# A two-layer graph network on one core: sums copied back over what they sum, and a reordered beginning

## The chip, the cores and the metric

The kernel runs on one core of a Trainium2 chip. The metric is the device time of one execution in microseconds (us); each kernel is run several times and the median is used. The engines are named as in the profile: PE is TensorE (matmuls; PEld are its weight loads), DVE is VectorE, ACT is ScalarE, POOL is GpSimd, and SP is SyncE, which here only issues transfers. Every engine works through its own list of instructions in order. Transfers issued by SP run on queue q1, those issued by POOL on queue q0; both share 16 DMA engines.

## The reference

`x` has 16 graphs of 1024 nodes with 256 channels; `adj` is one 1024 x 1024 matrix. All is float32.

```
h   = relu(layernorm(x))
c   = mean over channels of h                       # one number a node
Wg  = adj * A_s(c_m - c_n)                          # 1024 x 1024 for each graph
q   = relu((h^T Wg) * para)^T ;  k, v = h @ kv_w    # 4 heads of 64
x   = x + softmax(q k^T * scale) v
h   = relu(layernorm(x))
h1  = relu(batchnorm((A_hat h) @ W1^T + b1))        # statistics over all graphs
out = x + batchnorm(h1 @ W2^T + b2)
```

The softmax is taken without its maximum: exponentials are multiplied with the values, summed beside that, and the quotient is formed at the end.

## The kernel before, in words

The Python code emits all instructions itself, in the order in which each engine is to run them (`tc.manual_schedule()`); waits follow from the tiles' buffers. A pool with n buffers of a tag hands them round, and the first write into a reused buffer waits for the last use of its former tile.

**The beginning** (the `else` branch at the end of `layers`) is not overlapped with attention. `load_x(0)` brings graph 0 in two halves, after the small `vec`. `Norm` takes two row tiles at a time through `stats` (DVE), `scale` (POOL), `shift` (DVE) and `relu` (ACT), and `relu` also sums the channels into `csum`. `transposed` makes h^T on PE (L385) with a DVE copy (L388), half by half. `keys_values` is a generator of eight pieces: four products for the keys `pk` with an ACT copy each (L613), two for the first half of the nodes and two for the second, and four pieces for the values `pv` with DVE copies (L630). `differences(0)` spreads `csum` along rows: DVE copies (L190), PE transposes `cbp_c` (L201), ACT copies into `cbc` (L202). `weigh` then makes eight tiles `w`: absolute difference and tanh on ACT (L439, L447), product with a loaded tile of `adj` on DVE (L426), and for graph 0 a row sum of that tile (L429). `AHEAD = 6` steps of it are woven into the remaining pieces of `keys_values`. Then graphs 1 and 2 are loaded, and `plain_queries(0)` (16 pieces, `pg` and `q`, L593 and L596) runs with the rest of `weigh` and the first layer norm of graph 1 woven in from piece 5. `weave(main, (start, side))` takes one step of a side after every piece from number `start` on; what is left of a side follows the main part.

**Attention** runs over 64 units (graph, pair of heads `k`, half of the queries `f`), four steps each. A step emits `scores` (PE L871, exponential on ACT L879), `add` (DVE L898 and L901 add the exponentials into `acc`, two buffers), `values` of the step before (PE L912), and pieces of a background. When a unit ends, `sums` adds up `acc` over its partitions on PE (L929), copies the result to `row` on ACT (L931), and POOL stores it (L932) and loads it back, turned, as `inv` (L937). Two or three steps later `finish` transposes the unit's output and `add_output` takes the reciprocal of `inv` on DVE (L955) and adds the result to `x`.

The tile `row` comes from the pool `py`, which has four buffers under the tag `y`. Others use the same tag:

```python
                two = py.tile([P, 2, HB], F32, tag="y", name=f"two_{u}")
                one = py.tile([P, HB], F32, tag="y", name=f"one_{u}")
                y = py.tile([P, FB], F32, tag="y", name=f"y_{i}_{j}")
```

`two` and `one` belong to `graph()`, which runs once, in the background of graph 0: POOL loads blocks of `adj` (`au`, L247), combines them (L261 to L271) and writes them to DRAM (`aht_d`, L273 to L275), eight rounds in all. `degrees()` runs beside it: SP loads `at` (L206), ACT and DVE sum it (L221 to L229), and POOL takes a root (L84). All POOL work of these and of the units' sums stands in one queue.

Of the kernel before, what the change touches and what calls it, by code (L numbers as in the profile page):

```python
# [10 lines left out]
F32 = mybir.dt.float32  # L11
# [6 lines left out]
P = 128  # L18
# [5 lines left out]
def gnn_two_layers_kernel(  # L24
# [12 lines left out]
    nc = tc.nc  # L37
    B, N, C = x.shape
    H1 = w1_t.shape[1]
    NT = N // P  # L40
# [3 lines left out]
    FB = 512  # L44
# [10 lines left out]
    ident = const.tile([P, P], F32, name="ident")  # L55
# [1 line left out]
    neg_half = const.tile([P, NT], F32, name="neg_half")  # L57
    nc.gpsimd.memset(neg_half, -0.5)
    vec = const.tile([P, 18], F32, name="vec")
    nc.sync.dma_start(out=vec, in_=vecs)  # L60
    b1, g1, be1 = (vec[:, i * HC : (i + 1) * HC] for i in range(3))
    b2, g2, be2 = (vec[:, 3 * HC + i * CC : 3 * HC + (i + 1) * CC] for i in range(3))
    stats1 = const.tile([P, HC, B * NH, 6], F32, name="stats1")
# [22 lines left out]
    def layers(shifted):  # L86
# [13 lines left out]
        py = st.enter_context(tc.tile_pool(name=f"py_{kind}", bufs=4))  # L100
# [29 lines left out]
        def run(*parts):  # L130
            for part in parts:
                while advance(part) is not None:
                    pass
            while queue:
                queue.pop(0)()

        def weave(main, *sides):

            for i, cost in enumerate(main):
                for start, side in sides:  # L140
                    if i >= start:
                        cost += next(side, 0.0)
                yield cost
            for _, side in sides:
                yield from side
# [7 lines left out]
        def bank(name):  # L153
            return ps_mm.tile([P, FB], F32, tag="mm", name=name)
# [4 lines left out]
                r = slice(e * HW, (e + 1) * HW)  # L159
                nc.tensor.matmul(dst[r], left[:, r], right, start=start, stop=stop)  # L160

        def load_x(b):
            xs[b] = p3.tile([P, NT, C], F32, tag="x", name=f"x_{b}")
            for half in range(2):
                t = slice(half * NT // 2, (half + 1) * NT // 2)
                nc.sync.dma_start(
                    out=xs[b][:, t], in_=x[b].rearrange("(t p) c -> p t c", p=P)[:, t]
                )
# [8 lines left out]
            )  # L177
            return t

        load_x(0)  # L180
        kvw = const.tile([P, CC, 2 * C], F32, tag="kvw", name=f"kvw_{kind}")
        nc.sync.dma_start(out=kvw, in_=kv_w.rearrange("(k p) j -> p k j", p=P))
        rows = big.tile([P, NH, NT], F32, name="rows")
# [190 lines left out]
        def transposed(b, k, halves=range(NH)):  # L374

            h = hs["a", b]
            if 0 in halves:
                ht = p3.tile([P, N], F32, tag="ht", name=f"ht_{b}_{k}")
                hts.setdefault(b, []).append(ht)
            ht = hts[b][k]  # L380
            for g in halves:
                pt = bank(f"htp_{b}_{k}_{g}")
                for j in range(FB // P):
                    t = g * (FB // P) + j
                    nc.tensor.transpose(  # L385
                        pt[:, j * P : (j + 1) * P], h[:, t, k * P : (k + 1) * P], ident
                    )
                nc.vector.tensor_copy(ht[:, g * FB : (g + 1) * FB], pt)  # L388

        def differences(b):  # L390


            cbc = p1.tile([P, N], F32, tag="cbc", name=f"cbc_{b}")
            cbcs[b] = (
                cbc.rearrange("p (t q) -> p t q", t=NT)
                if b == 0
                else cbc.rearrange("p (q t) -> p t q", t=NT)
            )
            weighers[b] = weigh(b)
            if b == 0:  # L400
                broadcast_row(cbc, columns_of(csums[b], f"c{b}"), f"c{b}")
                return
            nc.sync.dma_start(out=csum_d[b].rearrange("(p t) -> p t", p=P), in_=csums[b])
            nc.sync.dma_start(
                out=cbc, in_=csum_d[b].rearrange("(o n) -> o n", o=1).to_broadcast([P, N])
            )
# [161 lines left out]
        def plain_queries(b):  # L568

            h = hs["a", b]  # L570
            qs[b] = [p4.tile([P, N], F32, tag="q", name=f"q_{b}_{k}") for k in range(CC)]
            for q in range(NH):
                cols = slice(q * FB, (q + 1) * FB)
                pgs = [bank(f"pg_{b}_{q}_{k}") for k in range(CC)]
                paras = []
                for k in range(CC):
                    paras.append(p2.tile([P, FB], F32, tag="para", name=f"para_{b}_{q}_{k}"))
                    nc.sync.dma_start(out=paras[k], in_=para[k * P : (k + 1) * P, cols])
                for th in range(NP):
                    i = q * NP + th  # L580
                    for k in range(CC):
                        for j in range(TH):
                            t = th * TH + j
                            product(
                                pgs[k],
                                h[:, t, k * P : (k + 1) * P],
                                weighted[b][i][:, j, :],
                                t == 0,
                                t == NT - 1,
                            )  # L590
                        if th == NP - 1:
                            dst = qs[b][k][:, cols]
                            nc.vector.tensor_mul(dst, pgs[k], paras[k])  # L593

                            soon(
                                lambda dst=dst: nc.scalar.activation(  # L596
                                    dst, dst, AF.Relu, scale=SCALE
                                )
                            )
                        yield 1.71  # L600
# [282 lines left out]
        class Unit:  # L883
# [39 lines left out]
            def sums(self):  # L923

                u = self.index
                pt = ps_t.tile([P, FB], F32, tag="t", name=f"sums_{self.name}")
                for e in range(2):
                    r = slice(e * HD, (e + 1) * HD)
                    nc.tensor.matmul(pt[r, :], ones, self.acc[:, e, :], start=True, stop=True)  # L929
                row = py.tile([P, FB], F32, tag="y", name=f"row_{self.name}")  # L930
                nc.scalar.copy(row, pt)  # L931
                nc.gpsimd.dma_start(  # L932
                    out=sums_d[u], in_=row.rearrange("(e r) c -> e r c", r=HD)[:, 0, :]
                )
                self.inv = p2.tile([P, FB // P, 2], F32, tag="inv", name=f"inv_{self.name}")
                for e in range(2):
                    nc.gpsimd.dma_start(  # L937
                        out=self.inv[:, :, e], in_=sums_d[u][e].rearrange("(j q) -> q j", q=P)
                    )
# [85 lines left out]
        with st:  # L1025
            if shifted:
                for b in range(B):
                    if b > 0:
                        load_x(b)
                    run(Norm(b, True).all())  # L1030
                    differences(b)
                    for k in range(CC):
                        transposed(b, k)
                    run(islice(weighers[b], AHEAD))
                    run(weave(plain_queries(b), (0, weighers[b])))
                    if b == 0:
                        run(degrees(), graph())
                        load_later()
                    run(keys_values(b))
                    shifted_attention(b)  # L1040
                    norm = Norm(b, False)
                    run(norm.all())
                    nc.gpsimd.dma_start(out=x1_d[b], in_=xs[b])
                    if b == B - 1:
                        attn.close()
                        turns.append(second(kind))
                    run(aggregate(b), hidden(b))
            else:
                norm = Norm(0, True)
                norm.stats(0, 1)  # L1050
                norm.scale(0, 2)
                for t in range(2, NT, 2):
                    norm.stats(t, t + 1)
                    norm.shift(t - 2, 2)
                    norm.relu(t - 2, t - 1)
                    norm.scale(t, 2)
                norm.shift(NT - 2, 2)
                norm.relu(NT - 2, NT - 1)
                products = keys_values(0)

                for k in range(CC):
                    transposed(0, k, (0,))
                run(islice(products, 2))
                for k in range(CC):
                    transposed(0, k, (1,))
                differences(0)
                run(weave(products, (0, islice(weighers[0], AHEAD))))
                load_x(1)
                load_x(2)
                run(weave(plain_queries(0), (0, weighers[0]), (5, Norm(1, True).all())))  # L1070
                attention()
                attn.close()
                turns.append(second(kind))
                run(aggregate(B - 1), hidden(B - 1))
# [324 lines left out]
```

## Time and profile before

| | us |
|---|---|
| median of three runs | 2637.73 (2637.07 to 2638.66) |
| the profiled execution | 2634.44, of which its span 2632.6 |
| PE busy | 2555.9 (97% of the span) |
| DVE, ACT, POOL busy | 1725.3, 1440.5, 547.9 |

The busy share of PE is an average over a beginning, a long steady part and an end. The view of stretches gives busy time by engine and the granted PE clock for chosen times; the view of waits tells what ended idle time; the timeline gives single instructions with the idle time ahead of them in brackets. Times in these views count from the start of the span.

### The profile page before, as it was taken

What the parts mean: (1) busy time and instruction counts of PE and PEld (TensorE: products, weight loads), DVE (VectorE), ACT (ScalarE), POOL (GpSimd) and SP (SyncE); (2) the same over time, 40 slices, a digit from 0 to 9 for tenths busy, and PEclk for the clock granted to TensorE, in tenths of its full rate; (3) what the DMA queues carried; (4) which work ended last, traced back from release to release, by engine and by line L of the source; (5) the groups of instructions that cost most, each with busy time, mean ns of one, the idle gap of its engine ahead of it and who ended that gap; (6) DMA issues with size and microseconds to landing.
All of it is one profiled execution on the core that took longest, in us unless ns stands there. A gap on an engine that the chain in (4) does not pass through costs nothing. (4 is left out here: it accounts for less than half of the span.)

```text
span 2632.6 us, 31894 instructions
## 1 busy us (share of the span) xinstructions
PE 2555.9 (97%) x11754; PEld 937.9 (36%) x11754; DVE 1725.3 (66%) x2736; ACT 1440.5 (55%) x1905; POOL 547.9 (21%) x648
## 2 busy tenths in 40 slices
PE   8979999999999999999999999999999999999995
PEld 3333333333333333333333333333333333334443
DVE  5647575766757675757667575757576675557675
ACT  5756464737364564647374645556464744335544
POOL 1361111011111111110111111111111112036653
PEclk9999999999999999999999999999999999999997
DMA  4463415252433324152524343342425233455559
GB/s 162 136 214 104 153 61 181 84 179 82 152 101 141 104 97 148 59 186 77 180 81 152 101 150 102 109 135 66 176 73 180 81 137 97 132 196 207 193 182 378
DMA packets 137188, 364.02 MB, mean 138 GB/s; under 512 B 21440, under 2 KB 38336, under 8 KB 130880
## 3 DMA queue, kind: packets, MB, share of 16 engines
q1 hardware_dynamic: 110272, 282.70, 31.5%
q0 software_dynamic: 26752, 79.20, 8.7%
q8 instruction: 95, 1.56, 0.3%
q14 instruction: 69, 0.57, 0.1%
HBM read 287.06 MB, written 74.78 MB: 137 GB/s over the span
## 5 line engine op out<-in xcount | busy, mean ns | idle before, releaser
L879 ACT ACTIVATE p<-sc 128x1024 f32<-128x1024 f32 x512 | 495.0, 1020 | 470.3 <-PE sc L871 464.1
L901 DVE TENSOR_TENSOR acc<-acc,p 128x1024 f32<-128x1024 f32 x384 | 470.8, 1226 | 222.4 <-ACT p L879 202.1
L871 PE MATMUL sc<-q,k 64*128 64x512 f32 x2048 | 511.4, 618 | 14.3 <-ACT p L879 14.3
L912 PE MATMUL o<-p,v 128*64 128x512 f32 x2048 | 497.0, 606 | 0.0
L160 PE MATMUL pg<-w,h_a 128*64 128x512 f32 x1600 | 358.1, 592 | 3.6 <-ACT k L613 1.9
L160 PE MATMUL pa<-aht,h_b 128*64 128x512 f32 x1536 | 343.5, 592 | 0.0
L871 PEld LDWEIGHTS sc<-q,k 64*128 64x128 f32 x2048 | 176.2, 186 | 336.8 <-issue 278.7
L439 ACT ACTIVATE w<-cbc,csum 128x512 f32<-128x512 f32 x256 | 293.5, 1198 | 0.0
L932 POOL DMA_DIRECT2D sums_d<-row x64 | 37.6, 587 | 1199.8 <-ACT row L931 1199.8
L160 PE MATMUL py<-at,w 128*64 128x512 f32 x1024 | 230.4, 592 | 0.0
L912 PEld LDWEIGHTS o<-p,v 128*64 128x64 f32 x2048 | 124.6, 136 | 294.6 <-issue 293.9
L426 DVE SCALAR_TENSOR_TENSOR w<-w,adj 128x1024 f32<-128x1024 f32 x128 | 157.9, 1234 | 89.2 <-ACT w L447 85.2
L160 PEld LDWEIGHTS pg<-w,h_a 128*64 128x64 f32 x1600 | 115.6, 137 | 231.7 <-issue 216.9
L160 PEld LDWEIGHTS pa<-aht,h_b 128*64 128x64 f32 x1536 | 110.4, 137 | 213.3 <-issue 201.0
L726 ACT ACTIVATE y<-py,vec 128x512 f32<-128x512 f32 x128 | 87.7, 685 | 149.0 <-PE py L160 125.1
L730 DVE BATCH_NORM_STATS2 stats<-y 128x6 f32<-128x512 f32 x128 | 85.5, 687 | 86.2 <-ACT y L726 86.2
L898 DVE TENSOR_TENSOR acc<-p,p 128x1024 f32<-128x1024 f32 x64 | 78.9, 1232 | 92.3 <-ACT p L879 92.3
L447 ACT ACTIVATE w<-w 128x1024 f32<-128x1024 f32 x128 | 135.2, 1056 | 1.8
L501 DVE TENSOR_TENSOR w<-w,w 128x1024 f32<-128x1024 f32 x112 | 132.9, 1218 | 1.5
L727 POOL DMA_DIRECT2D y_d<-y x128 | 70.2, 549 | 303.3 <-ACT y L726 302.1
L937 POOL DMA_DIRECT2D inv<-sums_d x128 | 98.4, 772 | 147.0 <-issue 63.3
L160 PEld LDWEIGHTS py<-at,w 128*64 128x64 f32 x1024 | 74.2, 137 | 145.2 <-issue 139.5
(151 smaller groups left out, 2822.0 us busy)
## 6 DMA issues: line engine op xcount, KB each, us to landing
aht<-aht_d SPq DMA_DIRECT2D x224, 512.0 KB, 6.3
adj<-in_adj_dram SPq DMA_DIRECT2D x128, 512.0 KB, 4.2
y_d<-y POOLq DMA_DIRECT2D x128, 256.0 KB, 2.6
yin_f<-y_d SPq DMA_DIRECT2D x32, 1024.0 KB, 6.3
x<-in_x_dram SPq DMA_DIRECT2D x32, 512.0 KB, 5.0
para<-in_para_dram SPq DMA_DIRECT2D x64, 256.0 KB, 3.9
x_d<-x POOLq DMA_DIRECT2D x16, 1024.0 KB, 10.4
xo_f<-x_d SPq DMA_DIRECT2D x32, 512.0 KB, 8.6
```

The source lines that it names most:

```text
L160: nc.tensor.matmul(dst[r], left[:, r], right, start=start, stop=stop)
L426: nc.vector.scalar_tensor_tensor(w, w, 1.0, a, op0=ALU.add, op1=ALU.mult)
L439: nc.scalar.activation(w[:, t, :].rearrange("p (t q) -> p t q", q=P), cbc[:, q * NT // NH : (q + 1) * NT // NH], AF.Abs, bias=csum[:, th * ...
L447: nc.scalar.activation(made[i], made[i], AF.Tanh, scale=-0.5 / C)
L501: nc.vector.tensor_sub(block(i)[part], block(x)[part], block(y)[part])
L726: nc.scalar.activation(y, made, AF.Identity, bias=b1[:, j : j + 1])
L730: nc.vector.bn_stats(stats1[:, j, i, :], y)
L871: nc.tensor.matmul(sc[:, e, :], ks[b][k][r, m * P : (m + 1) * P], qs[b][k][r, f * FB : (f + 1) * FB], start=True, stop=True,)
L879: nc.scalar.activation(pr, sc, AF.Exp)
L901: nc.vector.tensor_add(self.acc, self.acc, pr)
L912: nc.tensor.matmul(self.o[r, :], vs[b][k][:, m, r], pr[:, e, :], start=(m == 0), stop=(m == NT - 1),)
L937: nc.gpsimd.dma_start(out=self.inv[:, :, e], in_=sums_d[u][e].rearrange("(j q) -> q j", q=P))
```

## The change

It has five parts. The result of `sums` is copied into the first half of `acc` itself instead of a tile of `py`. At the very beginning PE transposes the identity 24 times into an unused bank. The input of graph 0 comes in four transfers of two row tiles instead of two of four, and `vec` is loaded after it and after `kvw`. The two pieces of `keys_values` for the second half of the nodes come ahead of `differences(0)` instead of behind it. The first layer norm of graph 1 is woven in from piece 10 of `plain_queries(0)` instead of piece 5; by the emitted order its last four row tiles then come to ACT behind the last queries, the last two of them directly ahead of the first exponential.

```diff
-    nc.sync.dma_start(out=vec, in_=vecs)
...
-        def load_x(b):
+        def load_x(b, parts=2):
             xs[b] = p3.tile([P, NT, C], F32, tag="x", name=f"x_{b}")
-            for half in range(2):
-                t = slice(half * NT // 2, (half + 1) * NT // 2)
+            for part in range(parts):
+                t = slice(part * NT // parts, (part + 1) * NT // parts)
...
-        load_x(0)
+        load_x(0, 4)
...
-                row = py.tile([P, FB], F32, tag="y", name=f"row_{self.name}")
+                row = self.acc[:, 0, :]
                 nc.scalar.copy(row, pt)
...
             else:
+                nc.sync.dma_start(out=vec, in_=vecs)
+
+                warm = bank("warm")
+                for i in range(24):
+                    j = i % (FB // P)
+                    nc.tensor.transpose(warm[:, j * P : (j + 1) * P], ident, ident)
                 norm = Norm(0, True)
...
                     transposed(0, k, (1,))
+                run(islice(products, 2))
                 differences(0)
                 run(weave(products, (0, islice(weighers[0], AHEAD))))
                 load_x(1)
                 load_x(2)
-                run(weave(plain_queries(0), (0, weighers[0]), (5, Norm(1, True).all())))
+                run(weave(plain_queries(0), (0, weighers[0]), (10, Norm(1, True).all())))
```

## The prediction

> **What bounds the kernel now.** I read the page's first part, then the view of stretches, the waits of PE and ACT, and the timelines around them.
>
> ```profile
> PE 2555.9 (97%) x11754; PEld 937.9 (36%) x11754; DVE 1725.3 (66%) x2736; ACT 1440.5 (55%) x1905; POOL 547.9 (21%) x648
> ```
>
> ```profile
> 0.00:60.00 60.00, 47.48 (x242) 20.01 (x244) 33.61 (x71) 33.51 (x65) 7.09 (x20) 1.00 0.44 150
> 60.00:104.00 44.00, 38.28 (x168) 12.68 (x166) 22.70 (x37) 35.40 (x47) 2.52 (x4) 0.96 0.37 119
> 104.00:200.00 96.00, 82.06 (x394) 30.01 (x392) 54.37 (x78) 55.41 (x71) 68.43 (x91) 0.95 0.61 203
> 328.00:2296.00 1968.00, 1965.65 (x9358) 693.34 (x9356) 1311.92 (x2069) 1087.61 (x1423) 286.72 (x394) 1.00 0.36 120
> ```
>
> The columns are length, busy time of PE, PEld, DVE, ACT and POOL, the PE clock, DMA. From 328 to 2296 us PE idles 2.4 us: nothing is to be had there. The change can touch 12.5 idle us before 60, 5.7 before 104 and 13.9 before 200. In the last of these POOL is busy 68.4 of 96 us, far above its share elsewhere.
>
> ```profile
> ACT row L931 <- POOL two L266: 13.4, 1, 13.4
> ACT row L931 <- DMA aht_d<-two: 8.9, 1, 8.9
> ```
>
> Twice the copy to `row` waits for a `py` buffer that `graph()` holds. ACT's exponentials stand behind it, and PE waits 1.69 us at 142.5 and 8.22 at 181.1. Now POOL, and what DVE and PE do with its result:
>
> ```profile
> 142.88 0.58 POOL L275 DMA_DIRECT2D aht_d<-one  x1
> 143.46 0.58 POOL L932 DMA_DIRECT2D sums_d<-row  x1
> 151.38 1.56 POOL L937 DMA_DIRECT2D inv<-sums_d  x2 [7.34 <-DMA sums_d<-row]
> ...
> 183.79 1.68 POOL L84 TENSOR_TENSOR deg<-deg,neg_half 128x8 f32<-128x8 f32 x1
> 185.44 0.64 POOL L932 DMA_DIRECT2D sums_d<-row  x1
> 187.43 1.54 POOL L937 DMA_DIRECT2D inv<-sums_d  x2 [1.35 <-DMA sums_d<-row]
> ```
>
> ```profile
> 193.26 0.20 DVE L955 RECIPROCAL inv<-inv 128x8 f32<-128x8 f32 x1
> ...
> 194.96 2.54 DVE L901 TENSOR_TENSOR acc<-acc,p 128x1024 f32<-128x1024 f32 x2
> ```
>
> ```profile
> 198.35 1.03 PE L929 MATMUL sums<-acc,ones 128*64 128x512 f32 x4
> ```
>
> The row copied at 138.9 is stored at 143.46, the one copied at 179.5 at 185.44: each time as soon as POOL ends the work ahead of it (L275, L84), without a wait for ACT. **POOL, not the copy, decides when `inv` returns.** DVE needs it at L955, L901 stands behind L955, and PE's next `sums` needs L901.
>
> **What the skill says.** The Trainium skill, "TensorE: Matmul & The Clock Gate", Part 1 (the clock gate), says that PE runs at half clock until a free-running window of about 3.4 us was busy, and again after an idle one. The trace agrees: `pk` begins at 11.58 and its weight loads come 0.86 us apart until 14.2, 0.43 from 14.87; after the 8.22 us wait the `sc` group takes 3.79 us instead of 1.99. Its Part 4 (PE-mode transpose) says that transposes don't count as busy. The trace differs: from 2564 to 2598, where PE does transposes alone (L1325), the clock is 0.99. So I let the 24 raise it. Part 1 also says that ACT and DVE are strict FIFO, as the stalls behind L931 and L955 show.
>
> **Part by part.** Input: without `vec` ahead, the first issue comes at 0.73 instead of 1.18 (0.45 us), and 262 KB of the 524 need not land first, at the 368 GB/s of 3.5 to 5.5 us another 0.7 to 0.9. The first stats start 1.33 earlier (5.43 before) and the first relu, R, at 6.44 instead of 7.77. Two more issues of 0.5 us and `vec` delay `kvw` by 0.5 and the first `adj` by 1.0 on SP; `adj` isn't used before 26.7.
>
> Idle transposes: they begin at about 1.5, when the identity is there. 16 at half clock took 3.67 us at the end (0.23 each), so 24 need at most 5.5 and end by 7.0, when the first real one could start (R + 0.75 = 7.2): no delay. But real transposes come only every 0.59 us with ACT until about R + 2.4, so the clock may fall again. With it full, the first keys end at R + 7.05; if a window falls, about R + 8.4; before R + 8.98.
>
> Keys ahead: 2 x 1.72 us of `pk` now stand ahead of `cbp_c`, while DVE's `cb_c` copies hide beside them. Counting on from the first keys: eight transposes and two copies to +2.15 (0.74 a copy), second keys from +1.4 to +4.85, ACT copy 0.6, last `cbp_c` at +6.05. It ends at R + 13.1 = 19.5, or 20.9; before 20.36. In DVE's order three `v` copies now stand ahead of the first L426: product three ends 5.45 after `cbp_c`, copy 0.75, L426 and L429 2.35, so the first `adj` buffer is free 8.55 later; before 29.06 - 20.36 = 8.7. That releases the fourth `adj`, the loads of x and para, and the fifth `adj`, for which DVE waited until 41.72. These bytes (3.67 MB) keep the queue full, so the 41.72 moves with it: earlier by 0.95, or later by 0.4.
>
> Layer norm behind: two pairs of stats (0.96 each) leave DVE's way after 41.72, and `q` is ready 6.25 later instead of 7.55. Of ACT's eight relus (0.59 each) the last two now stand just ahead of the first exponential: 1.2 us. From 41.72 to that exponential I get 6.25 + 12.24 (seven `pg` pieces) + 1.4 (L593, L596) + 1.2 = 21.1; before 21.15. **Nothing is gained.** Behind it on SP, `csum_d`, `cbc` and the next `adj` come 5 us later than 57.6 to 59.4; first used at 75.9 and 79.4, so hidden. Without that cover each us late would be one on ACT.
>
> So the beginning is worth s = 0, between -1 and +1. Up to 104 ACT sets the pace (35.4 of 44 us) and carries s on.
>
> Sums: both copies go at once; the 8.9 and 13.4 us end. `acc` is now held until POOL's store lands, and DVE's first add two units later waits for that: store landed by 151.4, next use 165.7, hidden by 14 us, and by 10 where 187.4 meets 197.8. Between 104 and 185 POOL's chain needs no result of the late copies, so it ends at 185.44 - s again. Its `inv` lands 2.9 us after the issue at 188.2: 191.1. From L955 to the end of L901 were 4.24 us, so `sums` runs at 195.35 instead of 198.35: **3.0 us gained, not the 12 of the stalls.** PE, with the 9.5 idle and 2.1 slow us behind 172.8 gone, is there by about 187 and waits 8 us: **what is late next is `inv`.** After such a wait the clock is down for half to one and a half windows, 0.9 to 2.6 us lost, I take 1.7. The `at` loads, no longer held by ACT, move from 140 to 146 up to 132 to 139: they may shorten the 7.34 us wait at 151.38 or lengthen POOL's waits for `au` before. I take 0.3 gained, bounds -2.7 and +6.0 (the wait falling to the 1.35 of the next row).
>
> Sum: 0 + 3.0 - 1.7 + 0.3 = 1.6 us. The profiled execution took 2634.44, 3.3 under the median of the runs; I take the difference over to the median: 2636.1.
>
> **The rivals.** *POOL gives way* (chance 0.23): the sums store meets no `at` loads, all 6.0 us come back, PE waits 2 to 3 us only and loses 0.8 of clock: 3.0 + 6.0 - 0.8 = 8.2, so 2629.5. For it: three `at` loads lie in that wait now. Against: `cbc` and two `adj` loads follow them on SP and move up into their place. *POOL's chain grows* (0.13): two `at` loads of 524 KB at 383 GB/s (5.5 to 11 us) put 2.7 us ahead of `au`, the beginning loses 0.8, the clock 2.5: 3.0 - 2.7 - 0.8 - 2.5 = -3.0, 2640.7. It decides from where delay and clock exceed the 3.0; more than 5.3 would need both windows of the first keys cold too. *The beginning does nothing and the copy still waits* (0.02): 2637.7; in the emitted order it waits for PE alone. My forecast, **POOL's queue sets the end**, has 0.62 and its own range 2632.5 to 2639.5.
>
> **The numbers.** A measurement here can tell about 0.2% (5.3 us) from no change. Faster by that: most of the first rival and an edge of mine, 0.24; slower: the tail of the second, 0.07; between: 0.69. The range reaches from the first rival to the second, 2629.5 to 2640.7.
>
> **What would show it.** Right: no ACT wait at L931, but a DVE wait of 6 us or more for `inv` at L955 near 185 and a PE wait at `sums` L929 near 190 with a dip of the clock; POOL's third L932 within 2 us of 185.4; the first exponential within 1 us of 62.9. Wrong: PE idle under 3 us between 160 and 200, or a first exponential before 60.

## The result, and the profile after

The changed kernel takes 2641.99 us (median of 14 runs, 2640.22 to 2645.14), the kernel before on the same chip 2637.6 (2634.14 to 2638.66). The ratio is 1.0018, with an interval of 1.0011 to 1.0026: **slower, by 4.4 us in the medians**, where 1.5 us of gain were forecast. The profiled execution took 2640.84, of which its span 2638.9. Line numbers in views of the changed kernel and of runs made from it are its own, mostly one less than before; those of runs made from the kernel before (`e1`, `e4`, `e9`, `e10`, `e13`, `e15`, `e17`, `e18`) are its.

The first part of the page, and the view of stretches with the columns of before:

```profile
PE 2562.8 (97%) x11778; PEld 943.3 (36%) x11778; DVE 1728.1 (65%) x2736; ACT 1441.1 (55%) x1905; POOL 551.4 (21%) x648
```

```profile
0.00:60.00 60.00, 52.56 (x276) 24.17 (x278) 34.92 (x72) 33.27 (x63) 7.10 (x20) 1.00 0.44 150
60.00:104.00 44.00, 37.13 (x164) 12.40 (x162) 22.05 (x35) 37.11 (x53) 3.17 (x5) 0.96 0.36 120
104.00:200.00 96.00, 78.85 (x380) 29.26 (x378) 53.10 (x75) 53.88 (x67) 71.28 (x91) 0.93 0.61 203
328.00:2296.00 1968.00, 1965.51 (x9362) 694.19 (x9362) 1313.16 (x2069) 1090.46 (x1426) 287.26 (x395) 1.00 0.36 120
```

The long part from 328 us is as it was. PE is busy 5.1 us longer before 60, and most of that are the idle transposes. The loss is between 104 and 200: PE idles 17.2 us instead of 13.9, its clock is lower, and POOL is busier by 2.9 us. The waits of that stretch, PE's and DVE's (total, times, longest):

```profile
PE sums L928 <- DVE acc L900: 17.9, 2, 9.5
```

```profile
DVE inv L954 <- DMA inv<-sums_d: 22.2, 2, 13.1
```

ACT's waits for a buffer at the copy are gone; in their place DVE waits for `inv`, and PE behind it at `sums`. That is the mechanism that was forecast. Now POOL, DVE and PE at the end of it, from their timelines:

```profile
148.83 0.58 POOL L274 DMA_DIRECT2D aht_d<-one  x1
149.41 0.58 POOL L931 DMA_DIRECT2D sums_d<-acc  x1
...
189.33 1.68 POOL L83 TENSOR_TENSOR deg<-deg,neg_half 128x8 f32<-128x8 f32 x1
190.97 0.64 POOL L931 DMA_DIRECT2D sums_d<-acc  x1
```

```profile
196.62 0.20 DVE L954 RECIPROCAL inv<-inv 128x8 f32<-128x8 f32 x1 [9.09 <-DMA inv<-sums_d]
...
198.33 2.54 DVE L900 TENSOR_TENSOR acc<-acc,p 128x1024 f32<-128x1024 f32 x2
```

```profile
201.02 1.98 PE L928 MATMUL sums<-acc,ones 128*64 128x512 f32 x4 [9.54 <-DVE acc L900]
202.75 7.49 PE L159 MATMUL pk<-ht,kvw_f 128*64 128x512 f32 x24
```

The third store of sums comes at 190.97, not at 185.4. What POOL does from its first store of sums to its third is called the chain from here on: it takes 87.6 us (from 103.35) instead of 80.8 (from 104.63). And behind PE's 9.54 us wait the clock is down: `sums` takes 1.98 us (1.03 before), `pk` 7.49 (5.32).

### The profile page after: what moved, and what is told of

Its sections match the earlier page's. It is cut to its first block, busy times and chain, and to the rows that moved or that the text cites. A ratio compares the mean times of both kernels' runs of the same rounds, so it can differ in the third digit from the quotient of the medians.

```text
span 2638.9 us, 31947 instructions
## 1 busy us (share of the span) xinstructions
PE 2562.8 (97%) x11778; PEld 943.3 (36%) x11778; DVE 1728.1 (65%) x2736; ACT 1441.1 (55%) x1905; POOL 551.4 (21%) x648
## 5 line engine op out<-in xcount | busy, mean ns | idle before, releaser
L900 DVE TENSOR_TENSOR acc<-acc,p 128x1024 f32<-128x1024 f32 x384 | 472.1, 1229 | 216.5 <-ACT p L878 195.8
L931 POOL DMA_DIRECT2D sums_d<-acc x64 | 37.6, 587 | 1202.1 <-ACT acc L930 1202.1
L425 DVE SCALAR_TENSOR_TENSOR w<-w,adj 128x1024 f32<-128x1024 f32 x128 | 157.5, 1230 | 91.9 <-ACT w L446 86.5
## 6 DMA issues: line engine op xcount, KB each, us to landing
x_d<-x POOLq DMA_DIRECT2D x16, 1024.0 KB, 10.6
```

The costliest lines, as they stand in the source:

```text
L425: nc.vector.scalar_tensor_tensor(w, w, 1.0, a, op0=ALU.add, op1=ALU.mult)
L900: nc.vector.tensor_add(self.acc, self.acc, pr)
```

## The experiments

My theory after this result: POOL's queue sets the end, as forecast, but the change also makes the queue's own work longer. The rivals: the loss comes from the beginning; or it comes from SP's loads, which now meet POOL's transfers.

### The two halves of the change alone

`e1` is the kernel before with the copy only, `e2` the changed kernel with the old tile for the copy.

```diff
-                row = py.tile([P, FB], F32, tag="y", name=f"row_{self.name}")
+                row = self.acc[:, 0, :]
```

> The kernel before with one part of the change: the sums are copied into acc; the beginning is untouched. Theory (POOL's queue sets when inv returns; without ACT's waits its chain from the first to the third store of sums grows from 80.8 us to 87.6 and PE waits at sums instead, with the clock falling twice): no ACT wait at the copy, chain 85 us or more, PE waits at sums of 15 us or more in all, and the 1.3 us that the beginning of the changed kernel gains is missing: 5 to 6.5 us slower than before, about 2643. Rival (the loss comes from the beginning, the sums are neutral): within 1.5 us of before.

Measured: 2639.29 us, ratio 1.0011 (1.0003 to 1.0019).

> The changed kernel with the sums copied to a tile of py as before; the beginning stays changed. Theory: the two ACT waits of 9 and 13 us at the copy are back, POOL's chain is back at about 81 us, the first exponential comes near 61.6: 1.3 us faster than before, 2636 to 2637. Rival (the beginning costs): slower than before by 3 us or more.

Measured: 2637.71 us, ratio 1.0005 (0.9997 to 1.0013). So the copy alone costs about 2.5 us, less than I expected. The beginning, from which I expected 1.3 us of gain, gives no change clear of noise; in its profile the clock fell at 10.4 us, the first exponential came at 63.44, and the chain is 83.6 us, not 81. The runs of `e1` spread over 8 us, from 2633.3 to 2641.5, and the profiled one was short: 2633.36 us, chain 80.6, although DVE and PE do wait there as forecast:

```profile
190.03 0.20 DVE L955 RECIPROCAL inv<-inv 128x8 f32<-128x8 f32 x1 [10.08 <-DMA inv<-sums_d]
```

```profile
194.42 1.97 PE L929 MATMUL sums<-acc,ones 128*64 128x512 f32 x4 [10.65 <-DVE acc L901]
```

So there is something that differs between executions.

### Is it the inverse that is late?

`e3` is the changed kernel with six steps instead of three between the sums of a unit of graph 0 and the use of its inverse; `e4` does the same to the kernel before.

```diff
-                        later_by = 3 if last.at[0] == 0 else 2
+                        later_by = 6 if last.at[0] == 0 else 2
```

> The changed kernel, in which the units of graph 0 are finished six steps after their end instead of three, so that DVE asks for inv some 17 us later; nothing else is changed. Theory (inv is late against its deadline, nothing else): DVE waits under 3 us for inv, PE's waits at sums (17.9 us) and the slow clock behind them (about 3 us) go, 17 to 21 us faster than the changed kernel, 2621 to 2625. Rival (POOL's long chain is needed in time by something else, or ACT bounds this stretch): less than 6 us faster, 2636 or more.

Measured: 2628.31 us, ratio 0.9972 (0.9963 to 0.9982), by the ratios some 12 us below the changed kernel, less than expected. PE waits no more than 1.1 us at `sums`. The chain is still 84.9 us long, but DVE no longer waits for `inv`; it waits for the hold on `acc` instead. DVE's waits in 100 to 240 us:

```profile
DVE acc L897 <- DMA sums_d<-acc: 12.7, 2, 9.6
```

The first addition of a unit writes the `acc` of two units earlier, which POOL's late store still reads. The prediction had found this wait hidden by 10 us or more; without the stall for `inv` that cover is gone.

> The kernel before with graph 0's units finished six steps after their end; the sums still go to a tile of py. Theory: the ACT waits at row stay (20 us or more), PE's wait of 8.2 us for the exponential stays, only the 2.5 us at sums goes: 1 to 4 us faster than before, 2634 to 2636.5; so the copy into acc and the later finish are worth far more together than apart. Rival (the later finish alone does it): 12 us or more faster.

Measured: 2635.24 us, ratio 1.0000 (0.9992 to 1.0008). In the kernel before, later use gains nothing, as ACT's copy goes on waiting for `py` (26.6 us in two waits).

`e7` takes the transfers of the sums from POOL's queue to SP's and changes nothing else:

```diff
-                nc.gpsimd.dma_start(out=sums_d[u], ...)
+                nc.sync.dma_start(out=sums_d[u], ...)
...
-                    nc.gpsimd.dma_start(out=self.inv[:, :, e], ...)
+                    nc.sync.dma_start(out=self.inv[:, :, e], ...)
```

> The changed kernel with the store of the sums and the two loads of their transposed form issued by SP instead of POOL; nothing else moves. Theory (POOL's queue holds the inverse back): the reciprocals of the first units no longer wait 13.1 and 9.1 us, no TensorE wait over 3 us stands at the sums between 160 and 205 us, the clock does not fall at 159 and 197, and the run takes 2626 to 2631 us. Rival: SP's queue is held too, by loads of the adjacency that wait for a buffer ahead of the sums' transfers, or it holds those loads back: then a wait of the same size appears at the reciprocal or at w*adj (L425), and the run takes 2636 to 2642 us.

Measured: 2620.22 us, ratio 0.9937 (0.9924 to 0.9951), more than I expected. The stretch from 104 to 200, and the two reciprocals from DVE's timeline:

```profile
104.00:200.00 96.00, 95.77 (x468) 34.75 (x468) 65.72 (x86) 71.98 (x90) 60.67 (x72) 1.00 0.64 209
```

```profile
147.96 0.19 DVE L954 RECIPROCAL inv<-inv 128x8 f32<-128x8 f32 x1
...
176.67 0.19 DVE L954 RECIPROCAL inv<-inv 128x8 f32<-128x8 f32 x1
```

PE is busy 95.77 of 96 us at full clock; the reciprocals come at 148 and 177 without a wait, against 159.4 and 196.6. This shows that the sums' place in POOL's queue, and not the copy, held this stretch.

### What makes POOL's chain longer?

`e5` weaves the degrees, with their SP loads, behind the graph's work, to test the loads; `e8` leaves out additions of DVE, to test the operations.

```diff
-                    plain_queries(1), (0, norm), (0, w), (5, graph()), (7, degrees())
+                    plain_queries(1), (0, norm), (0, w), (5, graph()), (16, degrees())
```

> The changed kernel with the degrees' loads and sums of graph 0 woven in from step 16 instead of 7, behind POOL's quarters of the adjacency instead of beside them; the rest stays. It asks why POOL needs 46.1 us from its first to its second store of sums in the changed kernel (38.8 before). Theory 'transfers': the loads of adj_t for the degrees share the DMA engines with POOL's own loads and stores (POOL's waits for the last transfer of a quarter are 5.6 us in sum, 1.2 before); then the second store comes at most 41 us after the first and the run takes 2636 to 2639 us. Theory 'operations': POOL's subtractions are stretched by VectorE's additions beside them, and the loads do not matter; then 43 us or more, and 2640 to 2643 us.

Measured: 2641.64 us (ratio 1.002, 1.0013 to 1.0027), second store 44.3 us after the first. That looks like a verdict for the operations, but it is none: SP still issued its loads of `para` and two of `at` at 115.6 to 118.3, ahead of POOL's stores at 118.5.

> The changed kernel once more, unaltered, for how far one profiled execution stands for the others. If the length of POOL's chain is a property of the program, the third store of sums comes 86 to 89 us after the first (87.6 in the first profile) and TensorE waits 8 to 10 us for its sums again. If it varies with the execution, the chain can take 82 to 86 us and the waits 4 to 8. The first exponential is expected at 61 to 62 us where the clock stays up in the beginning, and later than 62.5 where it falls once before 20 us.

Measured: 2644.17 us, chain 88.6 us, waits at `sums` 19.4 us in sum: the long chain came again. The first exponential came at 64.34 instead of 61.61; here the clock fell at 8.3 us, and stayed down until 15.1.

```diff
-                else:
+                elif self.at[0] > 0:
                     nc.vector.tensor_add(self.acc, self.acc, pr)
```

> The changed kernel without the running additions of the exponentials (L900) of graph 0: only the first two tiles of a unit are added, so graph 0's sums are those of a quarter of the keys; 24 VectorE additions of some 2.55 us go. Theory (VectorE's additions stretch POOL's subtractions where both run): POOL's operations between the first and the third store of sums take some 61 us instead of 64.5, single ones of 1.6 to 1.8 us are back at 0.73, the chain takes 82 to 84 us instead of 87.6, and the run 2636 to 2639 us. Rival (other VectorE work or the transfers stretch them): POOL's operations stay at 63.5 us or more, the chain at 86 or more, and the run at 2640 to 2643 us.

Measured: 2634.36 us (ratio 0.9988, 0.9981 to 0.9995), faster than expected, which also counts the work left out. POOL's groups by form between 104 and 192 us (busy, mean ns), in the changed kernel:

```profile
L269 POOL TENSOR_TENSOR au_f<-au_f 128x256 f32<-128x256 f32 x8 | 9.0, 1124 | 0.2
L265 POOL TENSOR_TENSOR two<-au_f 128x256 f32<-128x256 f32 x8 | 7.9, 982 | 0.5 <-DMA au_f<-in_adj_t_dram 0.4
L270 POOL TENSOR_TENSOR one<-au_f,two 128x256 f32<-128x256 f32 x8 | 7.3, 917 | 0.0
```

and in `e8`:

```profile
L269 POOL TENSOR_TENSOR au_f<-au_f 128x256 f32<-128x256 f32 x8 | 6.5, 810 | 0.1
L270 POOL TENSOR_TENSOR one<-au_f,two 128x256 f32<-128x256 f32 x8 | 6.0, 749 | 0.0
L265 POOL TENSOR_TENSOR two<-au_f 128x256 f32<-128x256 f32 x8 | 5.8, 728 | 1.5 <-DMA au_f<-in_adj_t_dram 1.5
```

These subtractions take 0.73 to 0.81 us on average without DVE's running additions, 0.92 to 1.12 with them; the fourth (L266) falls from 0.95 to 0.84. By the view of stretches POOL is busy 63.6 us of the chain instead of 69.7. The chain falls by only 3.6 us, to 84.0, since POOL's idle time in it grows from 17.9 to 20.4; and 1.6 of the 3.6 lie where the order of transfers, treated next, plays a part too. The Trainium skill, "GPSIMD Engine Reference", Specifications, says that POOL shares its SBUF interfaces with VectorE and contends with DVE instructions that have two SBUF inputs; L900 is such a one. The section gives no figure; in these runs an operation of 0.72 us takes up to 1.79.

### Why the short and the long chain?

`e13` adds the moved layer norm alone to `e1`, `e14` is the changed kernel with the layer norm at its old place, `e15` is `e1` again.

```diff
-                run(weave(plain_queries(0), (0, weighers[0]), (5, Norm(1, True).all())))
+                run(weave(plain_queries(0), (0, weighers[0]), (10, Norm(1, True).all())))
```

> The kernel before with the sums copied to the place of what they sum and the second graph's layer norm woven in from piece 10 instead of 5; the head is the old one. If the moved layer norm lengthens POOL's chain: first to third store 85 us or more (80.6 with the copy alone), and 2640.5 us or more. If the head does: 80 to 82 us and 2638.5 to 2639.5, as with the copy alone (2639.3).

Measured: 2640.31 us, ratio 1.0019 (1.001 to 1.0028), chain 88.0.

> The changed kernel with the second graph's layer norm woven in from piece 5, as before; the copy and the head (idle transposes, four loads, keys ahead) stay. If the head lengthens POOL's chain: 85 us or more, and 2640.5 to 2642.5 us. If the layer norm does: 80 to 82 us and 2637.5 to 2639. If the chain only depends on the moment at which POOL and VectorE meet, both kernels lie between, 82 to 86 us.

Measured: 2645.82 us, ratio 1.0039 (1.0025 to 1.0052), chain 87.9; its clock fell at 10.8 and at 48.4 us, and the first exponential came at 66.56. The time is above what was expected.

> The copy alone once more. If the chain is a property of the program: 80 to 81.5 us between the first and the third store of sums, as in its first profile, and a time near 2633. If it varies with the execution, as the spread of its times (2633 to 2641.5) suggests: 82 to 88 us and a time up to 2641.

Measured: 2632.85 us (a single run), chain 80.6. So it is not one half of the beginning: with either of them the profiled chain is long, with neither it is short, and some runs of `e1` take as long as those of the changed kernel. Set side by side, the profiles differ in one order. In the kernel before, POOL's first stores of `aht_d` stood ahead of SP's loads (a line of POOL's timeline and two of SP's):

```profile
117.87 0.78 POOL L273 DMA_DIRECT2D aht_d<-au_f  x1
```

```profile
119.05 0.34 SPq L206 DMA_DIRECT2D at<-in_adj_t_dram  x1
119.44 1.10 SPq L578 DMA_DIRECT2D para<-in_para_dram  x2
```

In the changed kernel they stand behind them:

```profile
116.73 0.34 SPq L205 DMA_DIRECT2D at<-in_adj_t_dram  x1
117.12 0.91 SPq L577 DMA_DIRECT2D para<-in_para_dram  x2
```

```profile
118.38 0.80 POOL L272 DMA_DIRECT2D aht_d<-au_f  x1
...
126.13 1.46 POOL L246 DMA_DIRECT2D au_f<-in_adj_t_dram  x2 [2.23 <-DMA aht_d<-au_f]
```

The 1 MB of loads goes first, and POOL's next load waits for the buffer that the stores read. `graph()` runs in eight rounds, called quarters in the expectations; count the second from the first store of `aht_d<-au_f` to the next one. In four profiles these loads begin 1.2 us behind the first store (before, `e1`, `e15`, `e17` below), and the second quarter takes 7.7 us. In nine, the last of them is issued 0.2 to 1.9 us ahead of it, and the quarter takes 11.2 to 11.8. With 2.4 us (`e8`) it takes 9.8, with 4.5 us (`e3`) 7.4; this fits loads that are nearly through by then, but was not tested apart.

`e16`, an edit of the changed kernel, and `e17`, one of the kernel before, were to force one order or the other; `e18` profiles the kernel before again.

```diff
-                    plain_queries(1), (0, norm), (0, w), (5, graph()), (7, degrees())
+                    plain_queries(1), (0, norm), (0, w), (5, graph()), (8, degrees())
```

> The changed kernel with the degrees woven in from piece 8 instead of 7, so that the third load of adj_t and the two of para behind it on SP come later. Theory (order of POOL's stores and SP's 1 MB of loads): these loads are issued behind POOL's first stores of aht_d, the wait at L246 is under 0.5 us, the second quarter takes 7.7 us instead of 11.4, the chain 83 to 85 us instead of 87.6, and the run takes 2636 to 2639.5 us. Rival (the chain is long because of POOL's operations alone): the quarter shortens or not, but the chain stays at 86 us or more, 2640.5 to 2643 us. If the loads are issued ahead of the stores all the same, the run says nothing of either.

Measured: 2642.16 us, ratio 1.0021 (1.0013 to 1.0029); the loads stood ahead of the stores all the same, quarter 11.6, chain 88.3.

`e17` has a 6 in that place.

> The kernel before with the degrees woven in from piece 6 instead of 7: SP's loads come earlier, ahead of POOL's first stores in every execution. Theory (order): the second quarter takes 11 to 12 us as in the changed kernel, the chain 83 to 86 us instead of 80.8, and the runs below 2634 us that the kernel before has now and then are gone: 2637 to 2640 us. Rival: the order does not matter, then the times stay as they are, 2631 to 2639 with a median of 2636 to 2637.5.

Measured: 2638.01 us, ratio 1.0005 (0.9996 to 1.0013); in the profiled execution (2634.73) the stores stood ahead. Neither edit moved the order, so they say nothing of it: that the order lengthens the chain rests on the profiles set side by side, not on a run that forced it.

> The kernel before once more, unaltered. If its usual execution has SP's loads ahead of POOL's stores, this one does most likely: second quarter 11 to 12 us, chain 82 to 84 us, time 2636 to 2638.5. If the first profile was the usual one: 7.7 us, 80.8, and 2634.

Measured: 2638.71 us, quarter 11.7, chain 85.1. **The same kernel has both orders**, and by its time the profile from which I predicted was of the rarer kind: of the 142 runs of the kernel before beside the changed one and these experiments, 28 lie below its 2634.44. Which order a run without a profile had isn't known. Of the 14 of the changed kernel none lies below 2640. Whether the changed kernel can have the other order stays open; no profile of it showed it.

The profiles can now be sorted by order. Busy is POOL's time in the chain by the view of stretches, idle the rest:

| Kernel | issued first | chain | busy | idle |
|---|---|---|---|---|
| before, first profile | stores | 80.8 | 66.2 | 14.6 |
| with the copy alone (`e1`, `e15`) | stores | 80.6, 80.6 | 70.0, 69.3 | 10.6, 11.3 |
| before, `e18` | loads | 85.1 | 65.9 | 19.2 |
| with the new beginning alone (`e2`) | loads | 83.6 | 65.7 | 17.9 |
| changed | loads | 87.6 | 69.7 | 17.9 |

The copy makes POOL busier by 3 to 4 us in either order. With the stores first, its waits shrink by as much and the chain stays as it was. With the loads first, they shrink by 1.3 us (against `e18`) or not at all (against `e2`), and the chain grows. Why they don't give way there isn't shown.

`e18` and the changed kernel thus have the same order. POOL's last quarter in `e18`, then in the changed kernel:

```profile
182.61 0.72 POOL L267 TENSOR_TENSOR two<-au_f,two 128x256 f32<-128x256 f32 x1
183.29 0.72 POOL L270 TENSOR_TENSOR au_f<-au_f 128x256 f32<-128x256 f32 x1
183.97 0.72 POOL L271 TENSOR_TENSOR one<-au_f,two 128x256 f32<-128x256 f32 x1
```

```profile
181.97 1.60 POOL L266 TENSOR_TENSOR two<-au_f,two 128x256 f32<-128x256 f32 x1
183.54 1.72 POOL L269 TENSOR_TENSOR au_f<-au_f 128x256 f32<-128x256 f32 x1
185.21 1.72 POOL L270 TENSOR_TENSOR one<-au_f,two 128x256 f32<-128x256 f32 x1
```

In the changed kernel DVE adds exponentials at that moment, then multiplies by `adj` (L425, 1.75 us instead of 1.23). In `e18` ACT's copy still waits for its buffer, so PE waits for ACT and DVE has nothing to add. DVE in the changed kernel, then in `e18`:

```profile
181.41 3.24 DVE L900 TENSOR_TENSOR acc<-acc,p 128x1024 f32<-128x1024 f32 x2 [0.32 <-ACT p L878]
184.58 1.75 DVE L425 SCALAR_TENSOR_TENSOR w<-w,adj 128x1024 f32<-128x1024 f32 x1
```

```profile
184.64 2.55 DVE L901 TENSOR_TENSOR acc<-acc,p 128x1024 f32<-128x1024 f32 x2 [12.06 <-ACT p L879]
...
196.86 0.19 DVE L955 RECIPROCAL inv<-inv 128x8 f32<-128x8 f32 x1
```

PE's timeline of `e18`:

```profile
184.66 3.38 PE L871 MATMUL sc<-q,k 64*128 64x512 f32 x8 [7.38 <-ACT p L879]
...
201.94 1.03 PE L929 MATMUL sums<-acc,ones 128*64 128x512 f32 x4
202.80 5.32 PE L160 MATMUL pk<-ht,kvw_f 128*64 128x512 f32 x24
```

The stall that the change removes was also a quiet time for POOL. And the slow clock of that stall fell on `sc` at 184.66, where ACT set the pace: it was busy without a gap from 183.10 to 199.07, so the slow `sc` shows in no later wait. `inv` is not waited for in `e18` at all: its reciprocal begins at 196.86 without a wait.

### With POOL out of the way

Once the sums' transfers are on SP, what are the parts worth? `e9` is the kernel before with the edit of `e7`, `e10` adds that of `e1`, `e7` above is the whole change, `e11` is `e7` without the idle transposes, and `e12` is `e7` with a load moved. The edit of `e12`:

```diff
                 load_x(1)
-                load_x(2)
                 run(weave(plain_queries(0), (0, weighers[0]), (10, Norm(1, True).all())))
+                load_x(2)
```

> The kernel before with the store of the sums and the loads of the inverse on SP, nothing of the change in it. Theory (POOL's queue holds the inverse, and that is the whole of what stands in the way at graph 0): the reciprocals wait no more, but ACT's copy still waits for one of the four small buffers that POOL's quarters hold, 10 to 20 us in sum, part of it on the path; 2625 to 2631 us, above the changed kernel on SP (2620.2). Rival: the ACT waits are as large as before (22) and cost what the inverse cost; then 2634 to 2637 us.

Measured: 2622.29 us, ratio 0.9945 (0.9931 to 0.9958). Better than expected: ACT's waits for a buffer fall to 5.5 us, and POOL ends its last quarter at 166.6 us, against 186.1 in `e18`.

> The kernel before with the sums copied to the place of what they sum, and their transfers on SP; the beginning is the old one. Theory: with POOL out of the way the copy is worth what its waits were, and the new beginning 0 to 1.3 us, so 2620 to 2622 us against 2620.2 with the new beginning. Rival: the new beginning is worth 2 us or more once nothing behind it absorbs it, then 2622.5 or more; or it costs, then below 2620.

Measured: 2620.78 us (2620.32 to 2621.83), ratio 0.9938 (0.9925 to 0.9952); the runs of `e9` on the same chip lie above (2622.1 to 2624.7), so the copy gains 1.5 us here. What the new beginning adds (`e7`, on another chip) is 0.3 us by the ratios, not clear of noise.

```diff
-                for i in range(24):
-                    j = i % (FB // P)
-                    nc.tensor.transpose(warm[:, j * P : (j + 1) * P], ident, ident)
```

> The changed kernel with the sums' transfers on SP and without the 24 idle transposes. Theory 'the clock': the clock comes up some 7 us later, the first pk takes about 6 us instead of 3.65, the last cbp_c ends 1.5 to 2.5 us later and the first exponential 1 to 2 us later; 2621 to 2623 us. Rival 'the loads': the fifth w*adj waits for its tile of the adjacency anyway (5.3 us at 41 us in the kernel on SP), the delay vanishes there; 2619.5 to 2620.5 us.

Measured: 2622.31 us, ratio 0.9943 (0.9929 to 0.9956). The first `pk` takes 5.25 us instead of 3.65, and the fifth `w*adj` (L425) came at 44.15 instead of 40.96 us. By the ratios the idle transposes are worth 1.6 us here, but the runs of `e7`, on another chip, overlap with these. `e10`, on the same chip and with the old beginning, is 1.5 us faster: without the idle transposes the rest of the new beginning gains nothing.

> The changed kernel with the sums' transfers on SP and the load of the third graph's x (1 MB) issued behind graph 0's queries instead of ahead of the fifth tile of the adjacency. Theory: VectorE's wait for that tile (5.3 us, landing at 41 us) shortens by the time of 1 MB at some 400 GB/s, 2.5 us; TensorE's wait at 41 to 44 us goes, the first exponential comes 1.5 to 2.5 us earlier, 2618 to 2619 us. Rival: the tile waits for its buffer and not for the bytes ahead of it, then no change (2620 to 2620.5).

Measured: 2618.94 us, ratio 0.9929 (0.9916 to 0.9943), the best of all. The first exponential came at 61.22 instead of 63.47 (in `e7` the clock had fallen at 43.3), and PE's wait of 2.8 us before 44 is 0.75; the fifth `w*adj` came at 40.64 although the last `cbp_c` ended 2.8 us later than in `e7` (22.60, as the clock had fallen at 8.3), so its tile did come sooner.

## Why the prediction was wrong

Its mechanism held, and for executions with the order of transfers of the first profile its sizes of the copy did too. In `e1` the third store comes at 184.75 (185.44 forecast), `sums` runs at 194.42 (195.35 forecast), the slow clock behind it costs 2.0 us (1.7 forecast), and the `sc` behind that begins 1.9 us earlier than before (1.6 forecast). Both profiles of the changed kernel have the other order, and there two terms were off. Against `e18`, which has that order too:

| Term | forecast gain, us | measured gain, us | from |
|---|---|---|---|
| beginning | 0 (-1 to +1) | +0.55 | first store of sums 103.90, now 103.35 |
| POOL's chain | +0.3 | -2.5 | 85.1, now 87.6 |
| from the third store to `sums` | 3.0 | 2.9 | 12.9, now 10.05 |
| clock behind the wait | -1.7 | -3.0 | `sums` to the next `sc` 6.1, now 9.15 |
| sum | +1.6 | -2.05 | spans 2636.9, now 2638.9: -2.0 |

- **Input and idle transposes.** The first relu came at 5.99 (6.44 forecast), the idle transposes ended at 6.33 (by 7.0). That they raise the clock held: the first `pk` takes 3.65 us, and 5.25 without them (`e11`). That the clock may fall again held too. The last `cbp_c` ended at 19.91 in the first profile (19.5 forecast) and at 22.70 in the second (20.9 forecast: 1.8 short), where `pk` is slow:

```profile
10.31 6.02 PE L159 MATMUL pk<-ht,kvw_f 128*64 128x512 f32 x16 [0.74 <-DVE ht L387]
```

- **Keys ahead, layer norm behind.** The fifth `w*adj` came at 41.03 or 43.76 (0.95 earlier or 0.4 later than 41.72 forecast), the first exponential at 61.61 or 64.34 (62.87 and 62.17 before). So in these profiles the beginning is worth between 1.3 us and a loss of 2.2: zero was a fair middle, the bounds too narrow.
- **The copy.** No ACT wait, DVE's wait of 9.09 us for `inv`, PE's of 9.54 at `sums`, a dip of the clock: all as written. That 3.0 us come back because L954 is no longer late was right to 0.1; in `e18`, as in the first profile, the reciprocal begins later than `inv` lands, behind other work of DVE.
- **POOL's chain: the step that failed.** "Between 104 and 185 POOL's chain needs no result of the late copies, so it ends at 185.44 - s again." It needs no result of them, and in `e1` and `e15` it takes as long as before. But the length of its operations depends on what DVE does at the same time: POOL is busy 69.7 us of the chain instead of 65.9 in `e18`, and its waits, 17.9 instead of 19.2, take in only a third of that. And the forecast started from a profile with the short chain: in `e18` that of the kernel before is itself 4.3 us longer. I had looked for what POOL waits for, and asked only whether loads would get in its way.
- **The clock: the second term that was off.** I took 1.7 with bounds of 0.9 to 2.6 us; it was 3.0. The clock was down for 10.2 us from 196.8; PE began at 201.02, so 6.0 us of that lay behind the wait: 1.8 of the prediction's windows of 3.4 us, not half to one and a half. Half the clock for 6.0 us is the 3.0. The first profile had such a fall of 10.2 us too, from 175.1, but only 4.3 of it lay behind PE's wait.
- **The rivals.** "POOL's chain grows" was the right side, at 2640.7, and its 2.7 us are near the 2.5 measured, but for another reason: it had `at` loads ahead of `au`. "POOL gives way" had 6.0 us come back from POOL's wait for its store of sums; the `at` loads did move up as forecast (all issued by 138.1, 145.6 before), but that wait fell from 7.34 to 5.99 only.
- **The base.** I carried the 3.3 us between the profiled execution and the median over as if they were spread evenly. They were mostly the chain itself: it is 4.3 us longer in `e18`, whose time is near that of most runs. A profiled execution below all the runs beside it should have been read as one of another kind.

The medians differ by 4.4 us, the spans of the like pair by 2.0, and those of `e18` and the second profile of the changed kernel by 5.4. That one has the clock's fall in the beginning (2.2 us at the first exponential); how often executions have it was not measured.

## What to carry to other kernels

When a stall is removed, ask not only what is late next but what the stalled engines will do in the time that comes free, and which engine on the critical path shares a port or a queue with them. A wait directly ahead of TensorE's dense work cost its slow clock as well here (3.0 us), while a slow clock where another engine set the pace did not show. And where a small result travels through a queue that is full of large work, moving its transfers to a queue with room can be worth more than the edits around it: here 15 us (`e9`), and about 2 more with the whole change beside it (`e7`). Take more than one profile of the kernel before you predict from it.

## What the runs showed of the hardware that I had not expected

- POOL's subtractions of 128x256 take 0.72 us alone and 1.6 to 1.79 where DVE's two-input operations run beside them; DVE's pay too (3.24 us for two instead of 2.54).
- Transposes of the identity alone bring the clock up: 24 of them from 1.44 us, full clock from 5.69, and from there on they start 0.11 us apart instead of 0.21. It can fall again while real transposes come 0.59 us apart, at 8.3 to 10.8 us, in some executions (`e2`, the second profile of the changed kernel, `e8`, `e12`, `e14`) and not in others.
- Two executions of one program can differ by 4.3 us in span (2632.6 and 2636.9); in their profiles one queue's loads are issued 1.2 us behind the other's stores, or 1.2 us ahead.
